# Two expert blocks a step in three layers, tokens turned a step ahead, and the next layer's keys and values moved ahead of a half's blocks

## Chip, cores and metric

The kernel runs on one core of a Trainium2 chip. The metric is device time in microseconds of one launch; of several executions the median counts. A profile is one further execution with the hardware profiler on.

## The reference

The input x is 4 batches of 512 tokens of 128 float32 numbers; a context of 4 x 154 rows of 128 is fixed for all layers. Four layers follow each other, each with a cross attention and a mixture of experts, both added to x after a layer normalisation:

```
x = x + xattn(layernorm(x), context)     # layer 0: similarity attention, one head
                                         # layer 1: 16 heads of 8 with a mask
                                         # layers 2, 3: 16 heads of 64
x = x + moe(layernorm(x))                # 8 experts
```

The experts differ. Layer 0: top 2 of 8, `((x W0 + b0) * silu(x W1 + b1)) W2 + b2`, hidden size 512. Layer 1: top 1 of 8 with a capacity of 321 tokens an expert (a token beyond it gets nothing), `gelu(x W1 + b1) W2 + b2`, hidden 512. Layer 2: top 2 of 8, `gelu(x w1) w2`, hidden 256, no biases. Layer 3: top 2 of 8, `relu(x W1 + b1) W2 + b2`, hidden 512. The chosen experts' results are added with softmax weights.

## The kernel before

**Data.** x stays in SBUF as four tiles (one a batch, 128 tokens on the partitions, four tiles of tokens each). All matmuls of the layers' main work are float32; one matmul in the program is two instructions in the trace, a weight load (PEld) beside each.

**A layer.** `attend_first` (layer 0) or `attend_all` (layers 1 to 3) does the attention of 4 batches x 4 tiles. Then the experts work on two halves of eight token tiles (two batches) each. Per half:

- `route(layer, half)` normalises x (L242), transposes it (L250), multiplies by the gate weights (L663), finds the top experts, and ranks each token among those of its expert with triangular matmuls (L690, L692). From this it makes a slot for each token and expert (`su`, L714), so that the tokens of an expert fill whole blocks of 128 rows, and the number of the expert of each block (`eb`). Each of 16 scatters (8 in layer 1; L719, an indirect DMA of GpSimd) writes 128 rows to `buf[half]` in DRAM.
- `experts(layer, half)` works through 23 blocks (15 in layer 1; a fixed number, the worst case). `load(g)` brings four blocks of tokens from `buf` (L836, on SP's queue; it waits for all scatters of its half), `tokens(g)` transposes them (L846) and copies them to `tokT`. `up(j)` loads the block's expert number into registers of SP and PE (L854), has SP fetch this expert's first weights and biases into a tile `w` (L862, 516 KB in layer 0, 258 in layers 1 and 3, 128 in layer 2), and multiplies (L873; 8, 4, 2 and 4 matmuls) into a PSUM tile `sc` of two banks. `down(j)` is issued one block later, behind `up(j + 1)`: activation with the bias from `w` to `hT` (Silu on ACT and a product on DVE in layer 0, L889 and L893; Gelu on ACT in layer 1, L895, and layer 2, L882; in layer 3 Relu of two columns of tiles on DVE, L899, and then of two on ACT, L901), the second matmul with the resident `w2` (L904), a copy to `ys` (L912) and a store to `ybuf[half]` (L913, on SP's queue).
- `gather` takes the results back by 16 (8) indirect DMAs of GpSimd (L937), each of which waits for all stores of its half, and `combine` adds them to x with the weights (L955, DVE).

**Order.** The calls are issued in this order: two blocks of half 0, the end of the last attention tile with its projection (L424) and residual, then the route of half 1 in turn with further blocks of half 0, the rest of half 0, then 9 blocks of half 1 (5 in layer 1), then the combining of half 0 in between two and two blocks, then `prepare` for the next layer with all its parts for batch 0 (normalise, transpose, keys L555, values L568 and L578, queries L591), then the rest of half 1. Half 1's gathers and combining run beside the next layer's attention. Within the expert part the engines' orders are then chosen by a scheduler with a timeline model, which takes the issue order as priority; within `attend_all` the order of PE, ACT (and DVE in layers 2 and 3) is as written. Each engine, and SP's and GpSimd's queue, works in order.

Scatters and gathers wait in a list, `rows_due`; `row_transfers(n, behind)` starts the next n and binds them to an instruction, so that in the blocks two follow each copy to `ys`.

**Buffers.** `w` has 3, `tok` and `tokT` 2 each, `hT` and `ys` 3, `sc`, `tr` and `av` (PSUM) 2 each. A buffer comes free when the last reader of its former contents is done, for `w` that is the activation in `down`, since the bias lies in it (in layer 2 the up matmuls).

Of the kernel before, what the change touches and what calls it, by code (L numbers as in the profile page):

```python
# [34 lines left out]
NF = (4, 4, 2, 4)  # L35

# [10 lines left out]
def tile_xattn_moe_stack(ctx: ExitStack, tc: tile.TileContext, a: dict, out: bass.AP):  # L47
# [221 lines left out]
    class Tile:  # L269
# [61 lines left out]
        def replicate(self):  # L331
# [5 lines left out]
            self.rep = p2.tile([P, self.nb, P], F32, tag="rep", name="rep")  # L337
# [197 lines left out]
    def attention64(b, gather_x, wq, wk, wv, wo, add):  # L535
# [51 lines left out]
        def queries(i):  # L587
            at.qT[i] = t = p3.tile([P, 8, P], F32, tag="t8", name="qT")
# [26 lines left out]
        at.parts = ((lambda: keys(0), lambda: keys(1)), (xn, values), (values_ends, xnT), ())  # L615
        at.queries = queries
# [205 lines left out]
    def experts(layer, half, routed, w2):  # L822

        ebs, _, scatters = routed
        nj, nf, nu = BLK[layer == 1], NF[layer], UPS[layer]
        pack = a[f"up{layer}"]
# [24 lines left out]
        def up(j):  # L851

            xT = toks[j // 4][:, (j % 4) * P : (j % 4 + 1) * P]
            e = nc.values_load(  # L854
                ebs[0:1, j : j + 1],
                engines=[mybir.EngineType.SP, mybir.EngineType.PE],
                min_val=0,
                max_val=E - 1,
                skip_runtime_bounds_check_because="a count of at most E - 1, by a minimum",
            )  # L860
            w = wff.tile([P, 1032], F32, tag="w", name="w")
            nc.sync.dma_start(w[:, 0:width], pack[bass.ds(e, 1), :, :].rearrange("o p n -> p (o n)"))  # L862
            sc = ps_sc()
            for u in reversed(range(nu)):
                for fc in range(nf):
                    at = (u * nf + fc) * P
                    if layer == 0:
                        dst = sc[:, u, fc * P : (fc + 1) * P]
                    elif layer == 3:
                        dst = sc[:, fc // 2, fc % 2 * P : (fc % 2 + 1) * P]  # L870
                    else:
                        dst = sc[:, 0, fc * P : (fc + 1) * P]
                    nc.tensor.matmul(dst, w[:, at : at + P], xT, start=True, stop=True)  # L873
            return e, w, sc
# [3 lines left out]
        def down(j, e, w, sc):  # L878
            hT = p3.tile([P, nf, P], F32, tag="hT", name="hT")
            products = []  # L880
            if layer == 2:
                nc.scalar.activation(hT.rearrange("p f t -> p (f t)"), sc[:, 0, 0 : nf * P], AF.Gelu)  # L882
            for fc in range(nf if layer != 2 else 0):
                up = sc[:, 0, fc * P : (fc + 1) * P]
                b0 = w[:, bias + fc : bias + fc + 1]
                if layer == 0:
                    g = p2.tile([P, P], F32, tag="eg", name="eg", bufs=4)
                    b1 = w[:, bias + nf + fc : bias + nf + fc + 1]
                    silu = nc.scalar.activation(g, sc[:, 1, fc * P : (fc + 1) * P], AF.Silu, bias=b1)  # L889

                    for other in products:
                        tc.declare_no_dep(silu.ins, other.ins, reason="distinct banks and gates")
                    products.append(nc.vector.scalar_tensor_tensor(hT[:, fc, :], up, b0, g, ALU.add, ALU.mult))  # L893
                elif layer == 1:
                    nc.scalar.activation(hT[:, fc, :], up, AF.Gelu, bias=b0)  # L895
                else:
                    up = sc[:, fc // 2, fc % 2 * P : (fc % 2 + 1) * P]
                    if fc < 2:
                        nc.vector.tensor_scalar(hT[:, fc, :], up, b0, 0.0, ALU.add, ALU.max)  # L899
                    else:  # L900
                        nc.scalar.activation(hT[:, fc, :], up, AF.Relu, bias=b0)  # L901
            y = ps_av()
            for fc in range(nf):
                nc.tensor.matmul(  # L904
                    y[:, 0:D],
                    hT[:, fc, :],
                    w2[:, bass.ds(e, 1), fc, :].rearrange("p o d -> p (o d)"),
                    start=(fc == 0),
                    stop=(fc == nf - 1),
                )  # L910
            ys = p3.tile([P, D], F32, tag="ys", name="ys")
            row_transfers(2, nc.vector.tensor_copy(ys, y[:, 0:D]))  # L912
            stores.append(nc.sync.dma_start(ybuf[half][j * P : (j + 1) * P, :], ys))  # L913
# [6 lines left out]
        for j in range(nj):  # L920
            this = (j, *up(j))
            if last:
                down(*last)
            last = this
            if j % 4 == 2 and j // 4 + 1 in loaded:
                tokens(j // 4 + 1)
                load(j // 4 + 2)
            yield
# [143 lines left out]
    def layer1_setup():  # L1072
# [25 lines left out]
        def prepare(b, found):  # L1098
# [15 lines left out]
            def keys_queries():  # L1114
# [6 lines left out]
                at.qT = p3.tile([P, S], F32, tag="t8", name="qT1")  # L1121
# [55 lines left out]
            at.parts = ((masks,), (xn, values), (xnT,), (keys_queries,))  # L1177
            at.queries = lambda i: None
# [160 lines left out]
    for layer in range(4):  # L1339
# [9 lines left out]
        first = Steps(experts(layer, 0, routed[0], w2)).step(2)  # L1349
# [7 lines left out]
        while not second.done:  # L1357
            second.step(2)
            first.step(2)
# [54 lines left out]
```

## Time and profile before

| | |
|---|---|
| three runs, us | 1287.0, 1288.27, 1281.15 (median 1287.0) |
| the profiled execution | 1280.46 us; its span, from first to last instruction, 1278.7 us; mean granted TensorE clock 0.931 |
| busy share of the span | PE 85%, PEld 70%, DVE 58%, ACT 45%, POOL 20% |
| DMA | 126.80 MB, mean 99 GB/s |
| layer 0, half 0 and half 1 (first up to last down matmul) | 104.2 to 182.4, 179.0 to 255.7 |
| layer 1 | 471.4 to 516.8, 522.8 to 564.5 |
| layer 2 | 792.1 to 839.0, 853.0 to 899.3 |
| layer 3 | 1133.8 to 1197.2, 1197.1 to 1250.4 |
| the chain that ended last | PE 56%, DVE 13%, DMA 12%, issue 7%, ACT 5%, POOL 4% |

The page gives busy time by engine, the span in 40 slices, the DMA queues, the chain of work that ended last, and the costliest groups of instructions by line; behind it the trace can be cut by window. "idle before, releaser" of a group is how long the engine stood still ahead of it and what ended that; "issue" is time in which the engine waited for nothing that the profile shows. PE is a matmul, PEld a weight load, SPq the queue of SyncE, from which all direct DMAs start; POOL is GpSimd. Times of an instruction in a fence are microseconds from the span's start.

### The profile page before, as it was taken

Reading aid. Unit: us, or ns where it says so; the run is one execution under the profiler, and the core shown is the slowest. Engines: PE = TensorE matmul, PEld = TensorE weight load, DVE = VectorE, ACT = ScalarE, POOL = GpSimd, SP = SyncE. Lnnn points to the kernel's source line nnn. Section 1 sums busy time; section 2 is a strip of 40 time slices with the busy share of each in tenths; the row PEclk is TensorE's granted clock in tenths of the full one; section 3 lists DMA queues with packets and bytes.
Section 4 is the critical chain, followed back from the end, with each engine's and each line's share of the span. In section 5 each row is a group of like instructions: output and inputs, shape, how many; then the busy total and the mean of one; then the engine's idle time right before and its main releaser. Section 6 shows DMA issues by size and latency. Waiting matters only on the chain.

```text
span 1278.7 us, 26797 instructions
## 1 busy us (share of the span) xinstructions
PE 1086.2 (85%) x9351; PEld 890.2 (70%) x9351; DVE 738.7 (58%) x2066; ACT 574.5 (45%) x2290; POOL 253.1 (20%) x281
## 2 busy tenths in 40 slices
PE   4778998977878789889999989857899999899881
PEld 3657998933444458777878777846778878789880
DVE  6565547566676764336666675414476576656442
ACT  2114333454554554465665555312666655533230
POOL 2050404032000201302000022153220000403424
PEclk8778999988898988899999999879899999999996
DMA  7024786621011124633112224454331111345761
GB/s 228 1 81 140 226 251 183 185 97 29 12 30 53 50 65 116 172 94 68 35 35 52 52 73 114 128 151 118 115 68 35 35 35 35 88 109 161 204 190 56
DMA packets 136995, 126.80 MB, mean 99 GB/s; under 512 B 13466, under 2 KB 116511, under 8 KB 136479
## 3 DMA queue, kind: packets, MB, share of 16 engines
q1 hardware_dynamic: 129695, 110.39, 30.9%
q0 software_dynamic: 7168, 14.69, 4.0%
q8 instruction: 77, 1.26, 0.4%
q14 instruction: 55, 0.45, 0.1%
HBM read 101.31 MB, written 23.72 MB: 98 GB/s over the span
## 4 chain that ended last, share of the span: by engine, by line
PE 56%; DVE 13%; DMA 12%; issue 7%; ACT 5%; POOL 4%; SPq 2%; POOLq 0%; DVEq 0%; ACTq 0%
PE sc L873 9%; PE tr L370 6%; PE av L904 6%; PE av L407 5%; PE sc L606 5%; DMA w<-in_up 5%; PE tr L424 5%; ACT probs L307 3%; PE sc L591 3%; DVE nm L293 3%; DMA yg<-ybuf,su 3%; POOL yg L937 2%; PE av L389 2%; PE sc L1159 2%; PE tr L357 2%
## 5 line engine op out<-in xcount | busy, mean ns | idle before, releaser
L307 ACT ACTIVATE probs<-sc,nm 128x154 f32<-128x154 f32 x768 | 286.9, 403 | 157.0 <-DVE nm L293 156.8
L873 PE MATMUL sc<-tokT,w 128*128 128x128 f32 x1528 | 211.7, 286 | 22.2 <-DMA w<-in_up 17.4
L873 PEld LDWEIGHTS sc<-tokT,w 128*128 128x128 f32 x1528 | 190.6, 198 | 35.6 <-DMA w<-in_up 11.4
L293 DVE TENSOR_REDUCE nm<-sc 128x6 f32<-128x924 f32 x144 | 142.7, 1007 | 74.0 <-PE sc L606 50.1
L904 PE MATMUL av<-w,hT 128*128 x1160 | 168.5, 281 | 4.8 <-DVE hT L893 3.0
L307 ACT ACTIVATION_READ_ACCUMULATOR probs<-sc,nm 128x1 f32 x768 | 168.2, 219 | 0.0
L937 POOL DMA_INDIRECT yg<-ybuf,su x112 | 106.4, 950 | 255.7 <-DMA rd<-rT 61.3
L904 PEld LDWEIGHTS av<-w,hT 128*128 128x128 f32 x1160 | 148.3, 194 | 11.7 <-DVE hT L893 4.1
L719 POOL DMA_INDIRECT buf<-xn,su x112 | 109.3, 976 | 226.0 <-DVE eb L742 84.8
L235 POOL TENSOR_TENSOR rstd<-ve,nhalf 128x4 f32<-128x4 f32 x32 | 33.1, 1035 | 537.7 <-DVE ve L233 451.5
L263 DVE COPY pT<-tr 128x512 f32<-128x512 f32 x160 | 107.0, 684 | 43.6 <-PE tr L370 37.7
L407 PE MATMUL av<-pT,vm 128*64 128x128 f32 (+1 forms) x1536 | 105.8, 284 | 22.1 <-DVE pT L263 21.9
L370 PE MATMUL tr<-ident,probs 128*128 128x128 f32 x768 | 121.6, 289 | 1.5 <-DVE rT L336 1.5
L370 PEld LDWEIGHTS tr<-ident,probs 128*128 128x128 f32 x768 | 84.9, 144 | 33.4 <-issue 21.6
L407 PEld LDWEIGHTS av<-pT,vm 128*64 128x64 f32 (+1 forms) x1536 | 64.1, 126 | 55.1 <-DVE pT L263 30.1
L889 ACT ACTIVATE eg<-sc,w 128x128 f32<-128x128 f32 x184 | 53.2, 368 | 87.5 <-PE sc L873 77.5
L606 PE MATMUL sc<-kT,qT 64*128 64x154 f32 x1024 | 86.4, 307 | 3.5 <-ACT probs L307 3.5
L912 DVE COPY ys<-av 128x128 f32<-128x128 f32 x168 | 48.1, 286 | 69.7 <-PE av L904 66.3
L893 DVE SCALAR_TENSOR_TENSOR hT<-sc,w,eg 128x128 f32<-128x128 f32 x184 | 56.2, 342 | 46.7 <-ACT eg L889 46.7
L606 PEld LDWEIGHTS sc<-kT,qT 64*128 64x128 f32 x1024 | 70.9, 188 | 14.4 <-issue 9.9
L591 PE MATMUL sc<-xnT,wq 128*128 128x128 f32 x512 | 69.6, 292 | 2.3 <-ACT probs L307 2.3
L591 PEld LDWEIGHTS sc<-xnT,wq 128*128 128x128 f32 x512 | 63.8, 202 | 7.6 <-issue 3.9
(255 smaller groups left out, 1455.2 us busy)
## 6 DMA issues: line engine op xcount, KB each, us to landing
w<-in_up SPq DMA_DIRECT2D x46, 516.0 KB
w<-in_up SPq DMA_DIRECT2D x76, 258.0 KB
rep<-rd SPq DMA_DIRECT2D x64, 256.0 KB
ybuf<-ys SPq DMA_DIRECT2D x168, 64.0 KB
tok<-buf SPq DMA_DIRECT2D x36, 256.0 KB
w<-in_down SPq DMA_DIRECT2D x3, 2048.0 KB
w<-in_up SPq DMA_DIRECT2D x46, 128.0 KB
buf<-zero SPq DMA_DIRECT2D x2, 1472.0 KB
```

The costliest lines, as they stand in the source:

```text
L263: return nc.vector.tensor_copy(o, i)
L293: nc.vector.tensor_reduce(self.at.heads(self.nm, g, n), self.sc[g][:, :, 0 : n * S2].rearrange("p j (s k) -> p j s k", s=n), AX.X, ALU.max ...
L307: nc.scalar.activation(self.pr[:, h, :], self.sc[g][:, j, s * S2 : (s + 1) * S2], AF.Exp, bias=self.nm[:, h : h + 1], accum_out=self.rs[:, ...
L370: nc.tensor.transpose(q[:, t * P : (t + 1) * P], self.pr[:, h, 0:P], ident)
L407: nc.tensor.matmul(av[rows, cols], v, self.pT[n][:, t, :], start=False, stop=last)
L424: nc.tensor.matmul(o[:, 0:D], self.aT[:, c, :], self.at.wo[:, c, :], start=(c == 0), stop=(c == self.nb - 1))
L591: nc.tensor.matmul(sc[:, c // 4, c % 4 * P : (c % 4 + 1) * P], wq[:, c * P : (c + 1) * P], at.xnT[:, i * P : (i + 1) * P], start=True, sto ...
L606: nc.tensor.matmul(sc[:, j, s * S2 : (s + 1) * S2], at.qT[i][rows, c, :], at.kT[rows, c, :], start=True, stop=True)
L719: ins = nc.gpsimd.indirect_dma_start(out=buf[half], out_offset=bass.IndirectOffsetOnAxis(ap=su[:, t : t + 1], axis=0), in_=xns[t // NI][:, ...
L873: nc.tensor.matmul(dst, w[:, at : at + P], xT, start=True, stop=True)
L904: nc.tensor.matmul(y[:, 0:D], hT[:, fc, :], w2[:, bass.ds(e, 1), fc, :].rearrange("p o d -> p (o d)"), start=(fc == 0), stop=(fc == nf - 1),)
L937: ins = nc.gpsimd.indirect_dma_start(out=yg[:, t, :], out_offset=None, in_=ybuf[half], in_offset=bass.IndirectOffsetOnAxis(ap=su[:, t : t ...
```

## The change

`PER = (1, 2, 2, 2)` sets how many blocks a step of `experts` takes: one in layer 0, as before, two in layers 1 to 3. There:

- one `w` tile (as large as before, 1032 columns) holds both blocks' weights, filled by two DMAs; one `sc` tile holds both blocks, a bank each; the number of buffers of either is the same, so they hold twice the blocks.
- layer 2's Gelu is one instruction over both banks; in layer 3 the first block's four Relus are all on DVE, the second's all on ACT; in layer 1 all are on ACT as before.
- the second matmuls of both blocks go into one `av` bank, one copy moves both to `ys`, one DMA stores both (64 KB each before), and that copy starts four scatters or gathers instead of two.
- `tokens(g + 1)` and `load(g + 2)` are issued at block 4g (with the step of blocks 4g and 4g + 1) instead of 4g + 2.
- the calls outside count in blocks as before (`step(2 // PER)`), save for the blocks of half 1 that precede the combining of half 0: 9, 3 x 2, 5 x 2 and 5 x 2 by layer instead of 9, 5, 9 and 9.

In all layers that have a next one, `prepare` of the next layer is called before half 1's blocks, with `early` parts there (keys and values of batch 0; for layer 1 masks and values) and `late` ones (normalise, transpose; for layer 1 keys and queries too) after the combining as before. `rep` has one buffer (2 before), `qT` two (3), `hT` four (3).

```diff
+PER = (1, 2, 2, 2)
...
-            self.rep = p2.tile([P, self.nb, P], F32, tag="rep", name="rep")
+            self.rep = p2.tile([P, self.nb, P], F32, tag="rep", name="rep", bufs=1)
...
-            at.qT[i] = t = p3.tile([P, 8, P], F32, tag="t8", name="qT")
+            at.qT[i] = t = p3.tile([P, 8, P], F32, tag="t8", name="qT", bufs=2)
...
+        at.early, at.late = (lambda: keys(0), lambda: keys(1), values, values_ends), (xn, xnT)
...
-        def up(j):
-            xT = toks[j // 4][:, (j % 4) * P : (j % 4 + 1) * P]
...
-            w = wff.tile([P, 1032], F32, tag="w", name="w")
-            nc.sync.dma_start(w[:, 0:width], pack[bass.ds(e, 1), :, :].rearrange("o p n -> p (o n)"))
-            sc = ps_sc()
+        def up(blocks):
+            w = wff.tile([P, 1032], F32, tag="w", name="w")
+            w = w[:, 0 : per * width].rearrange("p (b n) -> p b n", b=per)
+            sc = ps_sc()
+            es = []
+            for b, j in enumerate(blocks):
+                e = nc.values_load(
...
+                nc.sync.dma_start(w[:, b, :], pack[bass.ds(e, 1), :, :].rearrange("o p n -> p (o n)"))
+                es.append(e)
+            for b, j in enumerate(blocks):
+                xT = toks[j // 4][:, (j % 4) * P : (j % 4 + 1) * P]
+                for u in reversed(range(nu)):
+                    for fc in range(nf):
+                        at = (u * nf + fc) * P
+                        dst = sc[:, u if per == 1 else b, fc * P : (fc + 1) * P]
+                        nc.tensor.matmul(dst, w[:, b, at : at + P], xT, start=True, stop=True)
...
-            if layer == 2:
-                nc.scalar.activation(hT.rearrange("p f t -> p (f t)"), sc[:, 0, 0 : nf * P], AF.Gelu)
+            if layer == 2:
+                hT = p3.tile([P, 2, nf, P], F32, tag="hT", name="hT", bufs=4)
+                nc.scalar.activation(
+                    hT[:, 0:n].rearrange("p b f t -> p b (f t)"), sc[:, 0:n, 0 : nf * P], AF.Gelu
+                )
...
-                    up = sc[:, fc // 2, fc % 2 * P : (fc % 2 + 1) * P]
-                    if fc < 2:
-                        nc.vector.tensor_scalar(hT[:, fc, :], up, b0, 0.0, ALU.add, ALU.max)
+                    elif b == 0:
+                        nc.vector.tensor_scalar(hT[:, fc, :], sc[:, b, cols], b0, 0.0, ALU.add, ALU.max)
...
-            ys = p3.tile([P, D], F32, tag="ys", name="ys")
-            row_transfers(2, nc.vector.tensor_copy(ys, y[:, 0:D]))
-            stores.append(nc.sync.dma_start(ybuf[half][j * P : (j + 1) * P, :], ys))
+            ys = p3.tile([P, 2, D], F32, tag="ys", name="ys")
+            row_transfers(
+                2 * n, nc.vector.tensor_copy(ys[:, 0:n], y[:, 0 : n * D].rearrange("p (b d) -> p b d", b=n))
+            )
+            rows = ybuf[half][blocks[0] * P : (blocks[0] + n) * P, :]
+            stores.append(nc.sync.dma_start(rows.rearrange("(b p) d -> p b d", p=P), ys[:, 0:n]))
...
-        for j in range(nj):
-            this = (j, *up(j))
+        for j in range(0, nj, per):
+            blocks = tuple(range(j, min(j + per, nj)))
+            this = (blocks, *up(blocks))
...
-            if j % 4 == 2 and j // 4 + 1 in loaded:
+            if j % 4 == (2 if per == 1 else 0) and j // 4 + 1 in loaded:
                 tokens(j // 4 + 1)
                 load(j // 4 + 2)
...
+            at.early, at.late = (masks, values), (xn, xnT, keys_queries)
...
-        first = Steps(experts(layer, 0, routed[0], w2)).step(2)
+        first = Steps(experts(layer, 0, routed[0], w2)).step(2 // PER[layer])
...
-            first.step(2)
+            first.step(2 // PER[layer])
...
         got = gather(0, routed[0], stores)
-        second = Steps(experts(layer, 1, routed[1], w2)).step(9 if layer != 1 else 5)
+        if layer < 3:
+            at = prepare(0, found)
+            for part in at.early:
+                part()
+        second = Steps(experts(layer, 1, routed[1], w2)).step((9, 3, 5, 5)[layer])
...
-            second.step(2)
+            second.step(2 // PER[layer])
         if layer < 3:
-            at = prepare(0, found)
-            for parts in at.parts:
-                for part in parts:
-                    part()
+            for part in at.late:
+                part()
             at.queries(0)
```

## The prediction

> **What bounds the kernel now.** I read the page first: PE is busy 85% of the span, so on average it is the bound, and the question is only where it stands still inside the stages that the change touches. The groups part says what it stands still for there (columns: busy us, mean ns of one | idle before, its releaser); DMA issues gives the transfers behind it.
>
> ```profile
> L873 PE MATMUL sc<-tokT,w 128*128 128x128 f32 x1528 | 211.7, 286 | 22.2 <-DMA w<-in_up 17.4
> L904 PE MATMUL av<-w,hT 128*128 x1160 | 168.5, 281 | 4.8 <-DVE hT L893 3.0
> L719 POOL DMA_INDIRECT buf<-xn,su x112 | 109.3, 976 | 226.0 <-DVE eb L742 84.8
> w<-in_up SPq DMA_DIRECT2D x76, 258.0 KB
> ```
>
> The first matmul of a block (L873) is late by 22.2 us in all, mostly for its weights; the second (L904) is hardly late. Then I cut the span into expert stages (columns of the windows view: us, then busy us and instructions of each engine, PE clock, DMA share, GB/s). Layer 1's second half begins in the first row's gap, layer 2's in the second; the third row is the end of layer 3.
>
> ```profile
> 518.00:523.00 5.00, 2.12 (x9) 1.66 (x10) 0.69 (x1) 0.11 (x1) 0.00 (x0) 0.68 0.66 185
> 839.00:851.00 12.00, 0.00 (x0) 0.00 (x0) 0.29 (x1) 0.00 (x0) 5.88 (x7) 0.57 0.38 113
> 1227.00:1250.00 23.00, 21.19 (x178) 20.08 (x176) 10.00 (x33) 7.37 (x23) 0.00 (x0) 1.00 0.54 153
> ```
>
> For 12 us in layer 2 PE does nothing at all. Why is in the chain of waits (start, length, what). First layer 1, then layer 2:
>
> ```profile
> 514.09 3.92 DMA buf<-xn,su
> 518.09 2.75 DMA tok<-buf
> 520.88 1.97 PE tr L846 x8
> 522.85 3.71 PE sc L873 x16
> ...
> 555.89 2.62 DMA w<-in_up
> ```
> ```profile
> 845.75 2.23 DMA buf<-xn,su
> 848.12 2.93 DMA tok<-buf
> ...
> 866.57 2.27 DMA w<-in_up
> 869.33 2.40 DMA w<-in_up
> ...
> 888.83 2.12 DMA w<-in_up
> ```
>
> A half's blocks can't begin before GpSimd has scattered all its tokens (L719), the last write has landed and SP has loaded them back. Inside the half the chain then runs through w loads one after another. In layer 3 the same, up to the end of PE's work:
>
> ```profile
> 1229.47 2.80 DMA w<-in_up
> ...
> 1237.65 3.37 DMA w<-in_up
> ...
> 1244.36 2.80 DMA w<-in_up
> ```
>
> A load takes about 2.8 us to land, a layer 3 block only 0.89 + 0.89 = 1.78 us of PE (eight 111 ns matmuls up, eight down). With three one-block buffers, each free only when its block's activation has read its bias, the loop is buffer free, SP turn, 2.8 us, matmul, activation: about 2.1 us a block over 1227 to 1250. PE's idle time in the six half stages of layers 1 to 3, counted from the records, is 2.0, 1.9, 4.5, 8.0, 2.9 and 5.9 us: 25 us, and 16 us more lie between the halves of layers 1 (516.8 to 520.9) and 2 (839 to 851).
>
> **What the Trainium skill says.** [...] Trainium Kernel Development and Optimization, "Key Constraints": queues of SP, ACT and POOL share the same 16 DMA engines; so more w loads in flight compete with gathers. The trace of before shows no such delay by itself; between 1197 and 1227, with gathers under way, the DMA share is 0.77. TensorE: Matmul & The Clock Gate, "What's actually happening": after an idle window of about 3.4 us PE runs at half clock. The trace agrees: clock 0.57 in the 12 us gap, 0.68 in layer 1's, where 16 matmuls then take 3.71 us in place of 1.78. PSUM — Partial Sum Buffer, "PSUM bank collisions": two engines must not use one bank at once. That fits one block per bank in layer 3, DVE on one, ACT on the other.
>
> **Part by part.** The sum is against the profiled execution, 1280.46 us (span 1278.7 and 1.8 around it); the median, 1287.0, lies 6.5 us above, the fastest run 0.7; the same sum is taken from all.
>
> Layer 0: experts unchanged. Ahead of its second half now stand layer 1's masks (one SP issue of some 0.35 us, 315 KB, 1.3 us of bandwidth, and one DVE compare) and values (two matmuls, two DVE products). They join queues in which nothing waits longer than that: 0, at most 1 either way.
>
> Pairing, PE: same matmuls, same order inside a block: 0. ACT and DVE: layer 3's four Relus on each engine per block pair, 4 x 344 ns and 4 x 365 ns, 1.4 us under the next pair's 3.56 us: 0. Layer 1's eight Gelus 2.9 us, under 3.56. Layer 2's one Gelu of 512 columns instead of two of 256 (384 ns each): under the pair's 1.8 us. Fewer ys copies (a 289 ns copy of 128 columns becomes one of 256): not late today. If that cover went, the dearest is layer 1's Gelu, 1.1 us once at a half's end.
>
> SP: before, each layer 2 block needs 1.38 us there (block number 0.27, register work and semaphores 0.3, w issue 0.34, store with its semaphore 0.43), more than PE's 0.9. Two blocks need 2 x 0.95 + 0.43, so 1.17 us a block: 0.2 x 23 = 4.8 us less queue in a half, the only part that a deeper buffer doesn't give. Store waits (L913) queue ahead of w issues; now half as many, but a store waits for two blocks. What waits behind it is the w load for three steps later, so its cover is about 5 us in layer 3: 0.
>
> Depth: three buffers of two blocks cover 6 x 1.78 = 10.7 us in layers 1 and 3, three times a load; the 2.8 us vanish unless bandwidth is short. Layer 3 then asks 258 KB of weights plus 128 KB of tokens and results per 1.78 us, 222 GB/s. Layer 0, with 516 KB per load and the same three buffers, moves 226 and 251 GB/s in two slices of the page (128 to 192 us), and its L873 waits only 2.7 us for w. So I take the waits as gone; the other bound, no gain at all beside gathers.
>
> Where a wait goes, what is late next? The built program's order answers this. Each half's start hangs on projection, residual, router and scatters.
> - Layer 1: blocks ahead of the last projection rise from 4 up and 4 down to 8 and 6, 24 matmuls of 0.22 us: the chain starts 5.3 us later. Scatters come four per pair and the second group waits for a later ys copy (about 510.6 by this order), so they finish near 516, against 515.05 today, and the half starts at 521 to 522, about as now. But the next layer's keys and values (L555 2.5 us, L568 2.0, L578 1.0, with their copies on ACT and DVE, which have room there: 0.1 us of ACT in the gap), which held PE between 527 and 549, are then done while it waits, the clock is warm (the 3.71 us lose 1.5), and w waits of 3.35 and 2.62 us at 536 and 556 are gone. 5.5 + 1.5 + 4 of the 6, less 1 for the start and 1.5 for coarser steps: -8.5 (bounds -3 and -11).
> - Layer 2: ahead of the rank matmuls stand as many ups and fewer downs than before, ahead of the last projection 10 more matmuls (2.2 us), against a w wait of 2.84 at 805.41. Start of the half unchanged (-2 to +1): scatters at 16 x 1.257 us set it. Keys and values (the same 5.5 us, copies included) move into the 12 us gap, where no engine but GpSimd works. But the half then runs into its gathers on GpSimd: 856.9 to 876.7, after that normalisation until 879.6. PE reaches the xn transposes with 14 blocks done about 869 and stands until 881; nine blocks (0.9 each) and queries (3.5) bring the next layer's scores to about 893.5, against 897.6: -4 (-7 to -1).
> - Layer 3: the rank matmuls have 17 more matmuls (3.8 us) in front and a 2.8 us w wait less (1160.55): the second half starts where it did. From 1197 its floor is 23 x 1.78 + 6 x 0.45 of transposes = 43.6, so 1240.6. Gathers (1203.4 to 1223.5) pace DVE's combining, which stands between its hT; that costs about 3. PE ends near 1244, against 1250.4: -6.5 (-10 to -3). The 28 us of final gathers are untouched.
> - Tokens one step earlier: each of six transposes (0.45 us) waits for a load issued a group earlier, as before: 0, -1 to +1. rep and t8 buffers fewer, hT more: their readers are done in order already: 0 to +1.
>
> Sum: 0 - 8.5 - 4 - 6.5 = -19. Profiled execution 1261.5, median 1268; of these the second is my forecast.
>
> **Rivals.**
> A: all idle time goes. 25 us of waits and 5.5 us of keys and values in layers 1 and 2 each are hidden, less the 3 that combining costs in layer 3: -33, 1254. For: layer 0 with more bytes per load hardly waits. Against: layer 2's gather chain is no w wait.
> B: the GpSimd chains are the bound everywhere. Only the w waits after the last gather count: layer 1's 2.6 us, layer 2's three of about 2.1, layer 3's eleven blocks at 0.3, 12 us; the later chains above take some 4 back: -8, 1279. For: 20.1 us scatter and 20 us gather stretches span most of each half.
> C: slower. PE's queue is in order; the coarser steps put block work (5.3, 2.2 and 3.8 us, counted above) before the projection and rank of each layer. If these delays reach the scatters whole and the four-row groups wait for later copies (2 more each), the halves start 7, 4 and 6 us later, and only half the 19 is won: +7: 1294. It decides from the point where the chain delay exceeds the removed wait, about 3 us a layer. Against: in layer 2 and 3 the same chain waits for w today.
>
> **How the numbers follow.** Forecast 0.50 (1261 to 1275), A 0.17 (1245 to 1261), B 0.20 (1275 to 1285), C 0.13 (1285 to 1302). Half a per cent, 6.4 us, is about what a measurement of this kernel can tell from no change, so faster means under 1280.6, 0.50 + 0.17 + 0.12 of B = 0.79; slower means over 1293.4, 0.09 of C; the rest, 0.12, lies between. Leaving out a tenth at each end: 1250 to 1284.
>
> **What would show it.** Right: L873's idle for w under 8 us; PE busy with L555 and L568 inside layer 2's gap; in layer 3 pairs at 3.6 us after 1227. Wrong: layer 1's first tr L846 of the second half after 524 us relative to an unchanged layer 0; w loads over 6 us in layer 3; PE's wait for xn in layer 2 longer than 12 us; and if scatters begin over 3 us later in two layers, C is the case.

## The result, and the profile after

Over 20 runs each the changed kernel takes 1276.6 us and the kernel before 1284.4 us; the ratio is 0.9943, with a 95% interval from 0.9923 to 0.9962. That is 7.3 us less (4.9 to 9.9), where 19 were forecast.

The groups part of the changed kernel's page, in answer to the lines shown ahead of the change (L877 was L873, L916 was L904, L722 was L719):

```profile
L877 PE MATMUL sc<-tokT,w 128*128 128x128 f32 x1528 | 201.3, 286 | 8.7 <-DMA w<-in_up 3.6
L916 PE MATMUL av<-w,hT 128*128 x1160 | 155.3, 279 | 3.2 <-DVE hT L905 2.5
L722 POOL DMA_INDIRECT buf<-xn,su x112 | 109.6, 979 | 227.0 <-DVE eb L745 97.3
```

The waits that the change aims at are gone: L877 stands still 8.7 us instead of 22.2, 3.6 of it for weights instead of 17.4. So the question is where that time went. The windows view of the changed kernel over the gaps ahead of the second halves of layers 1 and 2, over a stretch inside layer 2's second half, and over the end of layer 3:

```profile
530.50:537.30 6.80, 4.35 (x21) 2.37 (x19) 1.66 (x4) 1.53 (x3) 0.01 (x1) 1.00 0.68 193
846.50:860.00 13.50, 2.95 (x10) 1.42 (x9) 1.39 (x3) 1.00 (x2) 6.71 (x7) 0.76 0.38 114
879.00:890.00 11.00, 0.83 (x5) 0.78 (x5) 6.19 (x24) 0.00 (x0) 7.15 (x8) 0.58 0.41 122
1227.00:1250.00 23.00, 22.55 (x191) 21.63 (x190) 12.97 (x43) 7.23 (x25) 4.62 (x5) 1.00 0.62 179
```

The gaps are there still, now with keys and values in them (in layer 2's, PE is busy for 2.95 us of 13.5). A new one of 10 us has come in layer 2 (third row), and layer 3's end is full (22.55 of 23 us, 21.19 before).

**How to set the two profiles side by side.** This profiled execution took 1282.5 us, the slowest of the 20; that of before 1280.5, faster than its median. Ends of spans tell nothing here. The stretch from layer 1's first attention scores to its last has the same instructions in every kernel of this study, and took 210.0 to 220.1 us over 20 profiles. Two of them, windows view:

```profile
265.00:475.70 210.70, 163.13 (x1303) 82.51 (x1301) 146.37 (x332) 109.50 (x527) 28.31 (x29) 0.94 0.18 49
```
```profile
266.00:486.50 220.50, 176.24 (x1298) 90.20 (x1295) 147.05 (x331) 109.61 (x526) 28.39 (x29) 0.87 0.17 47
```

DVE, ACT and GpSimd are equally busy in both (first: depth_only, second: free_rows, both below); PE needs 13 us more at a clock of 0.87 than at 0.94. So I measure each layer from its own last scores matmul. That takes out the clock of the attention, but not that of the expert part behind it. Positions in the records, in us behind it, for layer 1, and the points where layers 2 and 3 end:

| | before (two profiles) | after |
|---|---|---|
| layer 1: last projection | 17.0, 17.0 | 22.9 |
| experts chosen (`sel` written) | 29.1, 29.4 | 33.1 |
| rank matmul begins | 29.1, 29.4 | 36.8 |
| slots (`su`) | 32.5, 32.8 | 39.5 |
| last scatter ends | 48.7, 48.3 | 54.5 |
| second half's first up matmul | 56.5, 55.8 | 61.3 |
| next layer's first softmax | 98.3, 97.7 | 99.7 |
| layer 2: next layer's first softmax | 117.1, 116.3 | 111.0 |
| layer 3: last down matmul | 124.4, 124.4 | 116.2 |
| layer 3: end | 152.7, 152.7 | 145.9 |

Layer 1 lost 1.7 us, layer 2 won 5.7, layer 3 won 6.8: 10.8 in all, 3.5 more than the timed difference, within what its interval and one profile each leave.

The chain of waits shows layer 1's part. First the kernel before, then the changed one:

```profile
495.25 0.13 DVE sel L677
495.43 0.21 PE tr L690
...
499.20 1.03 POOL buf L719
```
```profile
505.07 1.74 PE tr L666 x8
...
508.53 4.41 PE sc L877 x22
512.97 0.20 PE tr L695 x8
...
515.95 1.03 POOL buf L722
...
519.81 0.96 POOL buf L722
520.77 4.75 issue
...
525.76 0.96 POOL buf L722
...
529.55 3.33 DMA buf<-xn,su
...
533.45 3.17 DMA tok<-buf
```

Before, the rank matmul ran the moment its input was written. Now 22 up matmuls of the first half stand ahead of it on PE's queue, 4.41 us at a mean granted clock of 0.60, while `sel` has been ready since 509.1. Later four scatters wait 4.75 us for the next pair's copy to ys, which itself waits for that pair's down matmuls on PE.

### The profile page after: what moved, and what is told of

The parts are those of the page before. It is cut to its first block, busy times and chain, and to the rows that moved or that the text cites. A ratio compares the mean times of both kernels' runs of the same rounds, so it can differ in the third digit from the quotient of the medians.

```text
span 1280.8 us, 26318 instructions
## 1 busy us (share of the span) xinstructions
PE 1089.4 (85%) x9351; PEld 896.9 (70%) x9351; DVE 731.6 (57%) x2012; ACT 565.3 (44%) x2264; POOL 253.6 (20%) x281
## 4 chain that ended last, share of the span: by engine, by line
PE 59%; DVE 12%; DMA 9%; issue 8%; ACT 5%; POOL 5%; SPq 2%; POOLq 0%; DVEq 0%
PE sc L877 11%; PE av L916 6%; PE tr L371 6%; PE sc L607 5%; PE av L408 5%; PE tr L425 5%; PE sc L592 3%; DMA yg<-ybuf,su 3%; POOL yg L953 3%; ACT probs L308 3%; DVE nm L294 3%; PE sc L1175 2%; DMA w<-in_up 2%; PE av L390 2%; PE tr L358 2%
## 5 line engine op out<-in xcount | busy, mean ns | idle before, releaser
L877 PE MATMUL sc<-tokT,w 128*128 128x128 f32 x1528 | 201.3, 286 | 8.7 <-DMA w<-in_up 3.6
L877 PEld LDWEIGHTS sc<-tokT,w 128*128 128x128 f32 x1528 | 189.0, 200 | 15.5 <-ACT eg L900 5.2
L916 PE MATMUL av<-w,hT 128*128 x1160 | 155.3, 279 | 3.2 <-DVE hT L905 2.5
L953 POOL DMA_INDIRECT yg<-ybuf,su x112 | 106.7, 952 | 246.5 <-ACT pT L267 59.9
L722 POOL DMA_INDIRECT buf<-xn,su x112 | 109.6, 979 | 227.0 <-DVE eb L745 97.3
L916 PEld LDWEIGHTS av<-w,hT 128*128 128x128 f32 x1160 | 141.9, 193 | 8.9 <-issue 4.7
L236 POOL TENSOR_TENSOR rstd<-ve,nhalf 128x4 f32<-128x4 f32 x32 | 33.0, 1032 | 547.3 <-DVE ve L234 429.6
L408 PEld LDWEIGHTS av<-pT,vm 128*64 128x64 f32 (+1 forms) x1536 | 63.8, 126 | 55.7 <-DVE pT L264 30.9
L592 PE MATMUL sc<-xnT,wq 128*128 128x128 f32 x512 | 73.6, 303 | 4.7 <-ACT probs L308 2.3
L592 PEld LDWEIGHTS sc<-xnT,wq 128*128 128x128 f32 x512 | 67.3, 212 | 10.2 <-issue 3.6
L425 PE MATMUL tr<-wo,aT 128*128 128x128 f32 x512 | 66.2, 284 | 1.6 <-DVE xnT L256 1.3
```

The costliest lines, as they stand in the source:

```text
L408: nc.tensor.matmul(av[rows, cols], v, self.pT[n][:, t, :], start=False, stop=last)
L425: nc.tensor.matmul(o[:, 0:D], self.aT[:, c, :], self.at.wo[:, c, :], start=(c == 0), stop=(c == self.nb - 1))
L592: nc.tensor.matmul(sc[:, c // 4, c % 4 * P : (c % 4 + 1) * P], wq[:, c * P : (c + 1) * P], at.xnT[:, i * P : (i + 1) * P], start=True, sto ...
L722: ins = nc.gpsimd.indirect_dma_start(out=buf[half], out_offset=bass.IndirectOffsetOnAxis(ap=su[:, t : t + 1], axis=0), in_=xns[t // NI][:, ...
L877: nc.tensor.matmul(dst, w[:, b, at : at + P], xT, start=True, stop=True)
L916: nc.tensor.matmul(y[:, b * D : (b + 1) * D], hT[:, fc, :], w2[:, bass.ds(es[b], 1), fc, :].rearrange("p o d -> p (o d)"), start=(fc == 0) ...
```

## Experiments

My theory after this was one of order: on PE's in-order queue the pairs bring block work ahead of layer 1's projection and rank matmuls, so that the half's start moves back by as much as the change wins. The first rival was the clock: the kernel wins what was forecast and loses it to a lower granted clock. The second, that the keys and values are all of the gain. The five groups ran on five chips, on one of which the kernel before took 1288 us and on four 1358 to 1371; ratios are to the kernel before on the same chip, and differences between kernels are taken inside a group.

### First group (before: 1359.3 us)

after_again is the changed kernel.

> The changed kernel once more, for a second profile and for a ratio beside the other kernels of this group. Both theories: 0.994 of before. Order theory (the pairs put block work ahead of layer 1's projection and rank matmuls): in layer 1 the slots of the second half (su) come 5 to 7 us later after the last scores of the attention than in the kernel before, and its first token transpose too. Clock theory (the changed kernel loses its gain because PE's granted clock is lower beside the same work): layer 1's stage is as long as before where the clock is the same, and the mean granted clock stays about 0.012 under that of before.

Measured 0.9899 (0.9857 to 0.9941), 1347.6 us. In layer 1 the last projection, rank, su and the second half's first up lie 22.9, 36.8, 39.5 and 61.4 us behind the last scores, as in the first profile to 0.1 us: that part comes back on another chip. The clock comes back with it, 0.50 from 29.5 to 36 us behind the last scores in both.

l1_single, the changed kernel with

```diff
-PER = (1, 2, 2, 2)
+PER = (1, 1, 2, 2)
-        second = Steps(experts(layer, 1, routed[1], w2)).step((9, 3, 5, 5)[layer])
+        second = Steps(experts(layer, 1, routed[1], w2)).step((9, 5, 5, 5)[layer])
```

> The changed kernel with layer 1 at one block a step, all else as changed. Order theory: layer 1's su and scatters come back to where they were, the keys and values still lie in the gap, so 5 to 7 us faster than the changed kernel: ratio about 0.989. Clock theory: layer 1's pairing is not what costs, ratio 0.993 to 0.996, about 3 us more w waits at most.

Measured 0.9889 (0.9847 to 0.9932): under after_again by 0.0010 in the ratios and 2.8 us in the medians, where 5 to 7 us were expected; the intervals overlap. su is back at 32.7, as the theory says, but the last scatter ends at 55.2 and the half starts at 64.1. That the scatters go two to a copy can't be the reason, since they do so in the kernel before. Two things differ from it: the early keys and values stand on PE among the first half's last blocks, and PE's stretch of half clock lies from 39.5 to 50 us behind the last scores, beside 29.5 to 36.5 in the kernel before. pair_l2 and pair_l3 below have the second without the first (single steps in layer 1, late keys, half clock from 40 to 49.5 and to 47): their second half starts at 60.1 and 59.4, beside 56.5 and 55.8 in the kernel before. So the start of this half moves by some 3 us between kernels with the same steps in layer 1; the clock is the likely reason, but no run shows it alone. The order of the chain is one cause, then, and not the only one.

pair_only, which issues all parts of `prepare` after the combining, as before:

```diff
-        if layer < 3:
-            at = prepare(0, found)
-            for part in at.early:
-                part()
...
-            for part in at.late:
-                part()
+            at = prepare(0, found)
+            for parts in at.parts:
+                for part in parts:
+                    part()
```

> The changed kernel with keys and values issued after the combining again, as before. Order theory: layer 2's gap of 12 us and layer 1's wait are empty again, 5.5 us of PE come back in layer 2 only in part, since PE waits there for the gathers anyway; in layer 1 the second scatter group no longer waits behind the key and value matmuls: about 0.997. A third view, that the whole gain is the early keys and values and the pairs give nothing: 1.000 or above.

Measured 0.9901 (0.9871 to 0.9930), by the ratios as fast as after_again; its median is 2.8 us lower, which lies within the spread of the runs.

early_only, the kernel before with

```diff
+        if layer < 3:
+            at = prepare(0, found)
+            for part in at.early:
+                part()
         second = Steps(experts(layer, 1, routed[1], w2)).step(9 if layer != 1 else 5)
...
-            at = prepare(0, found)
-            for parts in at.parts:
-                for part in parts:
-                    part()
+            for part in at.late:
+                part()
```

> The kernel before with only the early keys and values (masks and values for layer 1), one block a step everywhere. Order theory: layer 1 wins up to 5 us without paying for the pairs, layer 2 some 2 of 5.5 since it is held by its w loads: about 0.995. Third view (all of the gain is here): 0.993 or under. If early keys only delay blocks that are needed for the gathers: 1.000.

Measured 0.9996 (0.9967 to 1.0024). The second rival falls, and so does a good part of my forecast: the early keys and values give nothing that shows in the time, with the pairs or without. In layer 2 one sees why. The waits view of layer 2's second half (us in all, times, longest): the kernel before; pair_l2 below, which has pairs there and late keys; the changed kernel:

```profile
PE tr L250 <- DVE xn L242: 2.4, 1, 2.4
```
```profile
PE tr L251 <- DVE xn L243: 6.5, 1, 6.5
```
```profile
PE tr L251 <- DVE xn L243: 10.2, 1, 10.2
```

With early keys PE gets to the transposes of xn earlier, and waits 3.7 us longer for xn, which hangs on GpSimd's gathers; in this group the same wait is 3.1 us in pair_only and 6.0 in after_again. In layer 1 the early keys do fill a gap (PE idle between the last scores and the second half: 12.6 us in pair_only, 7.9 in after_again), but a gap that the pairs had widened first, from 7.0 in the kernel before. In these two profiles the next layer's first softmax comes 5.3 us earlier in layer 1 with early keys (100.3 against 105.6) and 4.5 us later in layer 2 (125.8 against 121.3), so that little is left of either.

### Second group (before: 1288.1 us)

before_again is the kernel before.

> The kernel before once more, for a second profile beside the ones of this group: 1.000. If the clock view of the first comparison is right (the first profile of before had luck with the granted clock in the stages that the change doesn't touch), then this profile's stretch from the first scores of layer 1 to the last is longer than the 213.2 us of the first one, by up to 6 us.

Measured 0.9994 (0.9968 to 1.0020). The stretch from layer 1's first scores to its last was 210.8 us, not longer than the first profile's 213.2: the first profile had no luck there, and the clock view loses that support.

pair_l1, pair_l2 and pair_l3 are pair_only with pairs in one layer alone; where layer 3 has single steps, it keeps the two banks and the two engines of before, and the number of half 1's blocks ahead of the combining goes with the steps:

```diff
-PER = (1, 2, 2, 2)
+PER = (1, 2, 1, 1)   # pair_l1; (1, 1, 2, 1) pair_l2; (1, 1, 1, 2) pair_l3
```

> Pairs in layer 1 alone, keys and values issued late as before. Order theory: su of layer 1's second half comes 5 to 7 us later after the last scores, the removed w waits (about 4 to 6 us) pay for it at best: 1.000, from 0.998 to 1.003. If my prediction's layer 1 term held without the keys, 3 us of gain: 0.9975. Clock view: within 0.002 of 1.000 too, but then with su unchanged.

Measured 1.0025 (1.0003 to 1.0046): 3.2 us lost. su at 39.5, first up at 61.6. The clock view wanted su unchanged, and falls for layer 1's su. The late start is not all the pairs' own, as pair_l2 and pair_l3 start at 60.1 and 59.4 without them.

> Pairs in layer 2 alone. The changed kernel's profile has layer 2's expert stretch 6.1 us shorter; with the keys back in the half's middle I expect 4 us: 0.997. If the pairs' gain is all in layer 3: 1.000.

Measured 0.9988 (0.9970 to 1.0006), 1.5 us won, no more than its interval; the next layer's softmax in its profile comes at 111.2, as in the changed kernel.

> Pairs in layer 3 alone. The changed kernel's profile has layer 3's expert stretch 6.8 us shorter and there are no keys to move in this layer: 0.9945. If the gain of pairs needs the slower chip's longer loads: 0.998 on a chip with short ones, 0.993 on one with long ones.

Measured 0.9923 (0.9897 to 0.9948): 9.9 us won, on the chip with the shorter times too. Last down at 117.2. The three ratios add up to 8.2 us won, against 7.3 for the whole change. That leaves nothing for the early keys, as far as three intervals of 2 to 3 us to either side can tell.

### Third group (before: 1370.1 us)

free_gathers, the changed kernel with

```diff
         got = gather(0, routed[0], stores)
+        if layer:
+            row_transfers()
```

> The changed kernel with the gathers of each first half in layers 1 to 3 not bound to the second half's copies to ys: they start when all stores have landed. Theory of the gates (PE's wait of about 10 us for xn in layer 2's second half is the whole reason why the early keys win nothing there, and it hangs on gathers that start only behind the second half's first ys copy): layer 2's gathers start up to 10 us earlier against the second half's first up matmul, PE's wait for xn falls from 10 us to under 3, and the ratio to before goes from the changed kernel's 0.994 to 0.987 or 0.988. Rival (the gathers only collide with the token and weight loads of the half, so what is won comes back as longer loads): 0.993 to 0.996.

Measured 0.9869 (0.9843 to 0.9894), without the changed kernel in this group. The wait for xn is gone from PE's list in layer 2's second half, but 7.4 us of L877 waiting for nothing that the profile shows stand there. They need not have come in its place: after_again, with its wait for xn of 6.0 us, has 9.2 us of the same kind at L916 in this stage. Over a whole profile PE has 12 to 46 us of it on the four slower chips, in every kernel, and 0.4 to 1.1 us in the six profiles with the shorter times. The next softmax comes at 119.2, against 125.8 in after_again and 121.3 in pair_only. Layer 3 gives some of that back: its last down lies at 136.6 to 138.1 in the seven profiles with free gathers, and at 132.4 to 134.3 in the first group's three with pairs and bound gathers. A gain is likely, its size is open.

free_rows, in addition:

```diff
             second.step(2)
+            if layer == 1:
+                row_transfers()
             first.step(2 // PER[layer])
```

> As the kernel before this one, and layer 1's eight scatters of the second half not bound to ys copies either. Theory of the order: su itself stays 39 us behind the last scores (it hangs on PE's queue, not on the scatters), but the scatters take 10 us instead of 15, so layer 1's second half starts 4 to 5 us earlier: 0.003 to 0.004 below the ratio of the kernel with only the gathers free. Rival (the second half of layer 1 is bound elsewhere): no difference between the two.

Measured 0.9902 (0.9879 to 0.9925), 6.0 us slower than free_gathers. The scatters end at 49.9 instead of 54.4, but the half's first up stays (63.5, 62.6): the first half's own blocks are done only at 58.8, against 54.4. PE ran at half clock from 47 to 54 in this profile and not in free_gathers', so the two differ in more than the edit. What can be said is that freeing the scatters from the copies won nothing here.

depth_only, the kernel before with

```diff
-            w = wff.tile([P, 1032], F32, tag="w", name="w")
+            if layer == 0 or j % 2 == 0:
+                wide.append(wff.tile([P, 1032], F32, tag="w", name="w"))
+            w = wide[-1][:, j % 2 * 516 : j % 2 * 516 + width] if layer else wide[-1]
```

> The kernel before with one thing of the change: in layers 1 to 3 two blocks share a w tile, so that six blocks' weights can be under way instead of three; steps, banks, activations, copies, stores and the place of the keys are as before. If the pairs' gain is the depth alone: layer 3 as with pairs (0.992 by itself), layer 1 without the loss of pairs, some 2 us won there, layer 2 little: 0.989 to 0.991. If the gain is in fewer copies, stores and SP turns: 0.998 to 1.000.

Measured 0.9923 (0.9899 to 0.9947). The wait for weights falls as in the changed kernel. From its page, and then from the lines view of layer 3's expert part in the kernel before, the changed kernel and depth_only:

```profile
L875 PE MATMUL sc<-tokT,w 128*128 128x128 f32 x1528 | 213.4, 289 | 9.9 <-DMA w<-in_up 3.6
```
```profile
L873 PE MATMUL sc<-tokT,w 128*128 128x128 f32 x368 | 50.8, 281 | 6.7 <-DMA w<-in_up 6.2 <-DVE tokT L88 0.2
```
```profile
L877 PE MATMUL sc<-tokT,w 128*128 128x128 f32 x368 | 46.0, 277 | 1.4 <-DVE tokT L89 0.8 <-DMA w<-in_up 0.6
```
```profile
L875 PE MATMUL sc<-tokT,w 128*128 128x128 f32 x368 | 51.3, 285 | 2.0 <-issue 1.7 <-DVE tokT L88 0.2
```

In layer 3 alone that is 6.2, 0.6 and, with depth alone, nothing of note. Layer 3's last down lies at 134.2, beside 132.4 to 134.3 in the first group's three kernels with pairs. The three profiles of the four slower chips that have neither pairs nor depth in layer 3 (early_only, and l1_order and pair_l1_b below) have it at 142.5 to 143.4. So layer 3's gain is the depth of the weight buffers, as the prediction's sum had it, and not the wider copies or stores. In layer 2 the next softmax lies at 132.4, against 121.3 to 125.8 with pairs and 134.8 in early_only: there depth gives little, and the pairs do. Whether they do it by fewer turns on SP's queue, as the prediction counted, was not tried by itself.

mixed_free is free_rows with layer 1 at one block a step and two blocks to a w tile there.

> Layer 1 one block a step with two blocks sharing a w tile, layers 2 and 3 in pairs as changed, gathers of layers 1 to 3 and layer 1's scatters not bound to ys copies. If the theories of the order and of the gates both hold: su of layer 1 back at 32 us behind the last scores, scatters 10 us long, layer 2's wait for xn gone: 0.980 to 0.984. If only the gates hold: 0.985 to 0.988.

Measured 0.9850 (0.9824 to 0.9875), 3.2 us under free_gathers by the medians of 5 and 6 runs, which overlap; at the edge of what the gates alone (gathers freed from the copies) would give and above what both theories would. su is at 32.4 and the scatters end at 42.7, yet the half starts at 60.0: its first half ends at 57.8.

### Fourth group (before: 1370.6 us)

l1_order is pair_l1 with an order on PE alone. `hold` is the last projection's matmul, and later the rank matmul:

```diff
-                        nc.tensor.matmul(dst, w[:, b, at : at + P], xT, start=True, stop=True)
+                        ins = nc.tensor.matmul(dst, w[:, b, at : at + P], xT, start=True, stop=True)
+                        if layer == 1 and half == 0 and hold:
+                            wait_for(ins, hold, "behind the chain of the next half")
```

> Pairs in layer 1 alone, as in pair_l1, but the up matmuls of all pairs after the first one are held behind the last projection on PE's queue, and those after the fourth behind the rank matmuls (an order on one engine, no new wait between engines). Order theory: su comes back from 39 us behind the last scores to 32 or less, the second half starts 4 to 6 us earlier than with pairs alone, and the loss of pair_l1 (1.0025) turns into a gain: 0.997 to 0.999. Rival (the scatters' binding to ys copies sets the start of the half, not the order): su comes earlier, the last scatter and the first token transpose do not, and the ratio stays within 0.001 of pair_l1_b.

Measured 0.9968 (0.9948 to 0.9988).

> Pairs in layer 1 alone once more, as the mark for l1_order on the same chip. Both views: 1.0025 as before, within 0.002.

Measured 1.0007 (0.9986 to 1.0027). So the order is worth 4.4 us by the medians of 22 runs each (0.0039 in the ratios). The chain of waits of pair_l1_b and then of l1_order, at the rank matmuls (L693 and L695):

```profile
511.82 4.53 PE sc L879 x22
516.38 0.20 PE tr L695 x8
```
```profile
508.90 0.13 DVE sel L680
509.03 0.05 issue
509.08 0.21 PE tr L693
509.29 0.19 PE tr L695 x8
509.47 3.68 PE sc L880 x32
```

The blocks now follow the rank instead of leading it. The clock moves with them (windows view, PEclk before the DMA's two numbers; pair_l1_b, then l1_order):

```profile
512.00:514.00 2.00, 2.00 (x10) 2.00 (x11) 0.38 (x4) 0.00 (x0) 0.00 (x0) 0.50 0.04 8
```
```profile
510.00:512.00 2.00, 2.00 (x21) 2.00 (x20) 2.00 (x17) 0.57 (x1) 0.00 (x0) 1.00 0.00 0
```

The 22 matmuls take 206 ns each, the 32 take 115, so by my estimate about 2 of the 8.8 us that su wins are clock; the rest goes with the order. Last projection 15.6 instead of 22.9, su 30.7 instead of 39.5, first up 57.8 instead of 63.8, next softmax 99.3 instead of 105.6. The rival's forecast, that the half would not move, fails.

order_free is free_gathers with this order, free_gathers_b is free_gathers.

> The changed kernel with layer 1's pairs ordered as in l1_order and the gathers of layers 1 to 3 free of the ys copies. If order and gates are both real and independent: 0.004 below free_gathers_b. If the order does nothing: the same as free_gathers_b.

> The changed kernel with free gathers once more. On a chip where the kernel before takes about 1285 us, theory of the gates: layer 2's gathers start right behind the scatters, 10 us earlier, PE's wait for xn (10 us in the changed kernel) goes, 0.987. On one where it takes about 1360 us: 0.987 as measured there already. Rival (collision with token and weight loads): 0.993 on the faster chip.

Measured 0.9803 (0.9761 to 0.9845) and 0.9847 (0.9806 to 0.9889), medians 3.9 us apart (6 runs each): the order is worth about the same on top of the early keys and free gathers. Its next softmax in layer 1 is at 96.0, against 99.4.

### Fifth group (before: 1357.7 us)

order_all_free is order_free with free_rows' edit; order_free_b is order_free.

> As order_free, and layer 1's eight scatters of the second half not bound to ys copies. If the binding is what is left: first scatter at 31 us behind the last scores instead of 35, last one at 41 instead of 51, second half of layer 1 starts 4 to 8 us earlier, ratio 0.003 to 0.005 below order_free_b. If PE's own work of the first half is what is left (it must be done by then anyway): scatters earlier, the half's first up matmul not, ratios within 0.002.

> The changed kernel with layer 1's order and free gathers once more. 0.980 as measured if the chip takes about 1360 us for the kernel before; on one that takes about 1285 us: the changed kernel's 0.994, less 0.004 for the order, less 0.004 to 0.006 for the gathers: 0.985.

Measured 0.9906 (0.9875 to 0.9937) and 0.9894 (0.9853 to 0.9935), medians 2.6 us apart the other way, no more than the runs' spread. The scatters end at 41.1 instead of 52.5, and the half starts at 60.8 instead of 59.5: its tokens are there at 50.4, but PE's blocks of the first half end only at 57.0 (52.5 in order_free_b), with half clock from 40 to 47 that order_free_b doesn't have there. With the order put right and the scatters free, PE's own work, at the clock it gets, is layer 1's bound. order_free was 0.9803 in one group and 0.9894 in another, so a ratio carries more from chip to chip than its interval says. It is below the kernel before in both; that it beats the changed kernel is not shown, since the two were not in one group, and rests on free_gathers and on the 3.9 us.

## Why the prediction failed, step by step

- **Layer 1, -8.5: failed.** The step is "so they finish near 516, against 515.05 today, and the half starts at 521 to 522, about as now". The 5.3 us by which the projection would move were counted rightly (measured 5.9). Wrong was that the scatters' waits for copies would swallow them: those copies stand on the same delayed queue. On top, the 22 up matmuls ahead of the rank were not counted for this layer, though for layers 2 and 3 they were. su came 7 us later instead of 5.3, the half started 5.1 later instead of 1. The forecast's own sign of being wrong came with it: the half's first token transpose begins 59.9 us behind the last scores instead of 54.6, which is 526 on the first profile's clock, past the 524 named. With that the next term fell too, "5.5 + 1.5 + 4 of the 6": from the half's start to the next softmax the changed kernel saves 3.5 us, not the 9.5 implied. The keys filled a gap, but one that the delay had opened. Measured, where -8.5 was forecast: +1.7 in the profile, +3.2 and +1.0 for the pairs alone in two groups. l1_order shows the cause by removing it. What stays argued is how much of the 5.1 us belongs to the clock, since kernels with single steps in layer 1 and late keys started up to 3.6 us later than the kernel before as well.
- **Layer 2, -4: about right.** 5.7 in the profile; pairs alone, timed, 1.5 (-0.8 to 3.9). The wait for xn was forecast from 869 to 881, 12 us, and measured at 10.2. But I gave the early keys a share in the gain, and none shows: the next layer's first softmax comes at 111.2 in pair_l2, with late keys, and at 111.0 in the changed kernel.
- **Layer 3, -6.5: right, a little small.** Last down 8.2 us nearer, end 6.8; pairs alone 9.9 (6.7 to 13.3). The second half takes 46.5 us (1204.6 to 1251.1) where 47 were forecast, 53.3 before, above a floor of 43.6. The mechanism, depth against a 2.8 us load, is confirmed by depth_only. Loads beside the gathers did grow (one of 4.13 us in the chain at 1229), but with six blocks under way PE's up matmuls waited for weights 0.6 us in the whole layer.
- **Layer 0, tokens, buffers, SP, activations, 0: nothing in the traces speaks against it**; they weren't tried one by one. (The four parts of SP's time in layer 2 add up to 1.34 us, not 1.38; nothing hangs on that.) No run put two engines on one PSUM bank.
- **Rivals.** B's size came, by another way: not GpSimd bound everywhere, but a loss in one layer against gains in two. C's mechanism is the one at work, in layer 1 alone. Its point of decision, "about 3 us a layer", fits all three layers: in layer 1 the chain had no w wait of that size to give back (the projection moved 5.9), in layers 2 and 3 it had, and there su came earlier (39.4 against 43.9 and 42.4 for the first scatter in layer 2) or about as before.
- **Still open:** how much free gathers are worth beside the changed kernel on one chip; what the waits are, 7.4 us among them, for which the profiles of the slower chips show no cause; and why layer 1's half clock comes at one of two places.

## What to carry to other kernels

In this kernel, work that was ready early filled PE's queue ahead of the one matmul that a long chain waited for. When a step is made coarser, count what then stands before each link of every latency chain on that engine, not only what the step itself saves. A gap in which an engine waits is worth something only to work that would otherwise lie on the path behind it: moved keys turned into a longer wait for xn. And if deeper prefetch is what is wanted, it can be had without coarser steps, with two blocks in a buffer.

## What the runs showed of the hardware

- PE's granted clock in the same instructions differs from execution to execution enough to hide this change: over 20 profiles, layer 1's attention took 210.0 to 220.1 us, and its length follows PE's busy time times (1 - clock), summed over 2 us windows (10.5 to 25.5 us; correlation 0.93).
- In the changed kernel's layer 1 the clock falls to 0.50 from 29.5 to 36 us behind the last scores. It did not take the idle of about 3.4 us that the prediction names: since the last scores PE's longest standstill had been 1.5 us. With single steps in layer 1 the first low stretch lies between 29.5 and 36.5 in some kernels (before, depth_only) and between 39 and 50 in others (early_only, l1_single, pair_l2, pair_l3).
- The kernel before took 1288 us on one chip and 1358 to 1371 on four. The first stretch and layer 1's attention are the same on all (pre-expert part 104 to 111 us); the time comes in layers 2 and 3: the attention of layer 3 takes 228 to 231 us on the first and 245 to 251 on the others. Why is not known. The instructions' own times are the same (median of a matmul record 275 ns on all, of a softmax activation 394 and 393 ns), and in the longer stretches engines stand with nothing that the profile shows: the experts' second matmuls stand still 3.2 to 5.8 us in the six profiles with the shorter times, and 26 to 45 us in the fourteen others, whatever the kernel.
